# Softmax sums in a fused attention and convolution kernel: accumulated by DMA from GpSimd's queue in place of VectorE

## The chip, the cores and the metric

The kernel runs on one core of a Trainium2 chip. The metric is device time in microseconds (us) of one execution, taken as the median of several executions. The engines named below are TensorE (PE, with its weight loads as PEld), VectorE (DVE), ScalarE (ACT), GpSimd (POOL) and SyncE (SP, which here only issues DMAs). Each engine works through its own queue of instructions in order; an instruction that waits for a semaphore holds everything behind it on that engine.

## What is computed

Sixteen images of 128 channels and 32x32 positions (N = 1024) pass through two layers in float32.

```
qkv    = einsum('bchw,oc->bohw', x, w_qkv) + b_qkv          # 4 heads, 128 channels each
scores = einsum('bnc,bcm->bnm', q, k) * c ** (-0.5)
attn   = softmax(scores, axis=-1)
out    = einsum('bnm,bmc->bnc', attn, v)
x1     = einsum('bchw,oc->bohw', out, w_out) + b_out + x
# layer 1: two quantized 3x3 convolutions, each with batch norm over all images, and a residual
out    = batchnorm(conv3x3(act_quant(x1), weight_quant(w1)))
out    = batchnorm(conv3x3(act_quant(out), weight_quant(w2))) + x1
```

There are 64 heads (16 images by 4). The softmax divides by a sum over 1024 keys for every query; how these sums are formed is what the change is about.

## The kernel before, in words

**Attention (most of the time).** The weights are folded beforehand, so a head needs one projection `u` (L498) of the image, the scores `x^T u`, their exponentials, and a product with projected values `vo` (L520). For 63 of the 64 heads the loop at L902 runs four steps per head (`NK` = 4). A step takes two blocks of 128 keys: `scores` (L543) issues four score products of 512 queries on PE, and ACT writes their exponentials into one tile `e` of seven 128x512 slots (L551). The product with the values is done with seven half-size products instead of eight, so VectorE forms three combined operands from the four exponentials: T3 (L554), T1 and T2 in one instruction (L555), and T4 (L558). `attend` (L567) then issues the seven products into four PSUM banks. It does so one step late: in a step PE runs the scores of step s and then the products of step s-1.

**The sums.** T3 is B12+B22, the sum for the second half of the queries, and T4+T3 is B11+B21, the sum for the first half. So the sums over keys need only the slots T4 and T3, which are neighbours (`mine`, 128x1024). VectorE adds those of steps 0 and 1 into `sides[g]` (L562), and those of steps 2 and 3 on top (L564). At the end of the head `sum_up` (L634) reduces `sides[g]` over partitions in groups of 32 with one transposing reduce (L625). `inverse_sums` (L637) finishes the sum over the four partition groups with small copies (L652), a reduce (L654), an add (L657), a reciprocal (L658) and copies (L660), and spreads it over the partitions with a transpose (L664, tile `rb`).

**The rest of a head's end.** ACT copies the four PSUM banks out (`evacuate`, L595). `combine` (L601) alternates between ACT and VectorE: ACT copies L605 to L607, VectorE L608, ACT L612, VectorE L613, ACT L615, VectorE L617 and L618. `normalise` (L667) multiplies by `rb` and adds to the image's `acc` (L673 to L679). After an image's fourth head SP stores `acc` to DRAM (L681), and the image goes through quantization (L256, L257), row transforms (L782), the first convolution and its statistics between the steps of the next image's heads.

**What sets the order.** A dictionary `later` holds the work of head ends and other stages by step and half step (`at`, L846), and `run` calls it. That is the order in which the program is written; the framework that builds it may place an instruction earlier or later in its engine's queue, as long as the dependences hold. PE's products are chained in written order (`product`, L400).

**Buffers.** `e` has two buffers, so the first exponential of step s waits until every reader of step s-2's `e` is done. `es` (the accumulator `sides[g]`) has one, `u` two, the score PSUM tiles three. Since a step has four score products, the fourth product of a step needs the PSUM tile of the first, and so waits for the first exponential of that step.

**After attention.** Convolution outputs `ys` of the first layer stay in SBUF, except those of the images in `AWAY` (9 to 14, L240), which are stored to the DRAM tensor `y1d` (L813) and loaded back in one transfer, `back` (L987), before the second convolution.

Of the kernel before, what the change touches and what calls it, by code (L numbers as in the profile page):

```python
# [9 lines left out]
F32 = mybir.dt.float32  # L10
BF16 = mybir.dt.bfloat16
AF = mybir.ActivationFunctionType
ALU = mybir.AluOpType
# [178 lines left out]
def fast_path(  # L192
# [18 lines left out]
    B, C, N = x.shape  # L211
# [25 lines left out]
    for n in range(2):  # L237
        nc.gpsimd.memset(late[n][:, 0:1], float((B - 1) * N))

    AWAY = range(9, B - 1)  # L240
    ys = [None if b in AWAY else keep.tile([P, N], F32, name=f"y{b}") for b in range(B)]
    pads = []
    for i in range(NPAD):
# [4 lines left out]
    def quantize(b, src, scale, bias, r0=0, r1=H):  # L248

        cut = slice(r0 * W, r1 * W)  # L250
        t = qtp.tile([P, (r1 - r0) * W], F32, tag="qt", name="qt")
        if b == B - 1 and scale == A_LEVELS and r1 == H:
            nc.vector.tensor_scalar(t, src[:, cut], scale, 0.0, ALU.mult, ALU.max)
        else:
            nc.scalar.activation(t, src[:, cut], AF.Relu, bias=bias, scale=scale)
        nc.vector.tensor_scalar(t, t, A_LEVELS, MAGIC, ALU.min, ALU.add)  # L256
        return nc.vector.tensor_scalar(  # L257
            pads[b % NPAD][:, r0 + 1 : r1 + 1, 1 : W + 1],
            t.rearrange("p (h w) -> p h w", w=W),
            MAGIC,  # L260
            None,
            ALU.subtract,
        )
# [32 lines left out]
    def statistics(b, n):  # L296
        for hf in range(NHF):
            last = nc.vector.bn_stats(place(n, b, hf), ys[b][:, ts(hf, HALF)])  # L298
        return last
# [20 lines left out]
    def bn_params(n):  # L320

        new = lambda what: keep.tile([P, 1], F32, name=f"{what}{n}")
        mv = keep.tile([P, 2], F32, name=f"mv{n}")
        nc.vector.bn_aggr(mv, late[n])
        mean, var = mv[:, 0:1], mv[:, 1:2]
        rt = new("rt")
        nc.scalar.activation(rt, var, AF.Sqrt, bias=eps, scale=ss[:, n : n + 1])  # L327
        v = new("v")
        nc.vector.tensor_scalar(v, var, ss[:, n : n + 1], BN_EPS, ALU.mult, ALU.add)
        r = new("r")  # L330
        nc.vector.reciprocal(r, rt)

        t = new("t")
        nc.vector.tensor_scalar(t, r, r, v, ALU.mult, ALU.mult)
        nc.vector.tensor_scalar(t, t, -0.5, 1.5, ALU.mult, ALU.add)
        scale, bias = new("scale"), new("bias")
        nc.vector.tensor_scalar(scale, r, t, gs[:, n : n + 1], ALU.mult, ALU.mult)
        nc.vector.scalar_tensor_tensor(
            bias, mean, scale, be[:, n : n + 1], ALU.mult, ALU.subtract, reverse1=True
        )  # L340
        return scale, bias
# [31 lines left out]
    with ExitStack() as ph:  # L373
        pool = lambda name, bufs, **kw: ph.enter_context(tc.tile_pool(name=name, bufs=bufs, **kw))
# [2 lines left out]
        up = pool("u", 2)  # L377
        vp = pool("vo", 5)
        ep = pool("e", 2)
        esp = pool("es", 1)  # L380
        avp = pool("av", 1)
        evp = pool("ev", 1)
        smp = pool("small", 4)
# [11 lines left out]
        xt, us, vos, es, sides, avs, psa, accs, evs = {}, {}, {}, {}, {}, {}, {}, {}, {}  # L395
        exps, sums_added, attended, quantized, pe = [], [], [], [], []
# [120 lines left out]
        B12, B11, B22, B21, T4, T3, T2 = range(7)  # L517
# [22 lines left out]
        def score(ps, b, g, j, queries, cut=slice(0, HALF)):  # L540
            halves(ps[:, cut], lambda t: xt[b][:, ts(2 * j + t, PH)], us[g][:, queries])

        def scores(g, k, between=None):  # L543


            b, h = heads[g]
            e = es[g, k] = ep.tile([P, 7, HALF], F32, tag="e", name=f"e_{g}_{k}")
            for i, (c, m) in enumerate(((0, 1), (1, 1), (0, 0), (1, 0))):
                ps = ps_s.tile([P, HALF], F32, tag="s", name=f"pss_{g}_{k}_{i}")
                score(ps, b, g, k + NK * c, ts(m, HALF))  # L550
                exps[:] = [nc.scalar.activation(e[:, 2 * c + 1 - m], ps, AF.Exp).ins]  # L551
                if between and i in between:
                    between[i]()
            nc.vector.tensor_tensor(e[:, T3], e[:, B12], e[:, B22], ALU.add)  # L554
            nc.vector.tensor_tensor(  # L555
                e[:, T1 : T2 + 1 : T2 - T1], e[:, B12 : B11 + 1], e[:, B11 : T3 + 1 : T3 - B11], ALU.subtract
            )
            nc.vector.tensor_tensor(e[:, T4], e[:, T2], e[:, B21], ALU.add)  # L558
            mine = e[:, T4 : T3 + 1]
            if k == 1:  # L560
                sides[g] = esp.tile([P, NHF, HALF], F32, tag="es", name=f"es_{g}")
                nc.vector.tensor_tensor(sides[g], es[g, 0][:, T4 : T3 + 1], mine, ALU.add)  # L562
            elif k > 1:
                added = nc.vector.tensor_tensor(sides[g], sides[g], mine, ALU.add)  # L564
                sums_added[:] = [added.ins]

        def attend(g, k):  # L567
            b, h = heads[g]
# [231 lines left out]
        def rows_output(b):  # L800
            inner, others = ms.pop((b, True)), ms.pop((b, False))
            if b in AWAY:
                ys[b] = stp.tile([P, N], F32, tag="y", name=f"y_{b}")
# [6 lines left out]
        def first_statistics(b):  # L810
            statistics(b, 0)
            if b in AWAY:
                nc.sync.dma_start(out=y1d[b - AWAY.start], in_=ys[b])  # L813

# [31 lines left out]
        def at(step, half, fn, *args):  # L846

            later.setdefault(2 * step + half, []).append((fn, args))
# [21 lines left out]
        for g in range(LAST):  # L870
            b, h = heads[g]

            end = (g + 1) * NK
            at(end, 0, sum_up, g)
            at(end, 1, evacuate, g)
            at(end + 1, 0, combine, g, 0)
            at(end + 1, 1, combine, g, 1)
            at(end + 2, 0, combine, g, 2)
            at(end + 2, 1, normalise, g)
            if g > 0:  # L880
                at(g * NK + 1, 0, project_u, g + 1, 0)
                at(g * NK + 2, 0, project_u, g + 1, 1)
            if h == NH - 1:
                at(end + 3, 0, lambda b: quantize(b, accs[b], A_LEVELS, 0.0), b)
                at(end + 3, 1, sums_range, b)
                at(end + 4, 0, transform_rows, b)
                for i, k in enumerate((1, 2, 0, 3)):
                    at(end + 6 + (i + 1) // 2, (i + 1) % 2, rows_product, b, k)
                at(end + 8, 1, rows_output, b)
                at(end + 9, 0, first_statistics, b)  # L890
                if b + 2 < B:
                    at(end + 5, 0, load, b + 2, nc.scalar)
            elif h == NH - 2 and b + 1 < B:

                when = ((4, 0), (4, 1), (6, 1), (7, 0), (7, 1), (8, 0), (8, 1), (9, 1))
                for i, (step, half) in enumerate(when):
                    at(g * NK + step, half, project_v, b + 1, *divmod(i, 2))
# [4 lines left out]
        for step in range(n_steps):  # L902
            g, k = divmod(step, NK)
            between = {}
            if step == 1:
                banks = [ps_a.tile([P, HALF], F32, tag=f"a{2 + c}", name=f"psv_0_{c}") for c in range(2)]
                between = {0: lambda: project_v(0, 0, 0, banks[0]), 1: lambda: project_v(0, 0, 1, banks[1])}
            scores(g, k, between)
            if step == 0:
                fold_b()  # L910
            elif step < NK:
                project_v(0, step, 0)
            run(step, 0)
            if step > 0:
                attend(*divmod(step - 1, NK))
            if 0 < step < NK:
                ps = ps_s.tile([P, HALF], F32, tag="s", name=f"psv_0_{step}_1")
                project_v(0, step, 1, ps)
            run(step, 1)
# [31 lines left out]
    with ExitStack() as ph:  # L951
        pool = lambda name, bufs, **kw: ph.enter_context(tc.tile_pool(name=name, bufs=bufs, **kw))
# [32 lines left out]
        scale1, bias1 = bn_params(0)  # L985
        back = resp.tile([P, len(AWAY), N], F32, name="back")
        nc.sync.dma_start(out=back, in_=y1d.rearrange("b c n -> c b n"))  # L987
        for i, b in enumerate(AWAY):
            ys[b] = back[:, i]
# [203 lines left out]
def attention_then_quantized_convs(  # L1193
# [49 lines left out]
    def conv_weights(n, wp, behind):  # L1243
# [19 lines left out]

    flag = const.tile([1, 1], mybir.dt.int32, name="flag")
    fast_path(
        nc, tc, x, wqk, wvo, bo, bnp, x1d, y1d, out, bo_sb, bnp_sb, quad, wq, sc, flag, conv_weights,
        constants,
# [82 lines left out]
```

## Time and profile before

| what | value |
|---|---|
| three executions | 2024.09, 2026.29 and 2023.94 us; median 2024.09 us |
| span of the profiled execution (first to last instruction) | 2022.7 us |
| mean granted TensorE clock | 0.993 |
| PE busy | 1987.6 us (98%) |
| DVE busy | 1722.2 us (85%) |
| ACT busy | 1198.5 us (59%) |
| POOL busy | 19.7 us (1%) |
| DMA | 43.74 MB, mean 22 GB/s |

The profiled execution is one execution with its span; its own total time is not listed apart from the three runs, which lie 1.2 to 3.6 us above the span. A line of the page's table of groups names source line, engine, operation, output and inputs, count, busy time in us, mean ns of one instruction, and the idle time of the engine ahead of it. A line of the timeline gives start in us, length in us, engine, source line, operation and count, and in brackets how long the engine had been idle and who released it. A line of the waits gives who waited for whom, the total in us, the number of times and sometimes the longest.

### The profile page before, as it was taken

To read this page: it belongs to the slowest core of one execution; us is meant where nothing else is said; L and a number is where in the kernel's file an instruction comes from. 1 tells how busy PE (TensorE), PEld (TensorE's weight loads), DVE (VectorE), ACT (ScalarE), POOL (GpSimd) and SP (SyncE) were. 2 spreads that over 40 slices of the span, in tenths; PEclk is the share of its full clock that TensorE was granted. 3 is DMA by queue.
4 is the path that set the end of the run, shared out by engine and by line. 5 is a ranking of instruction groups with operands and counts; after the bars stand their busy time and mean duration, and the time that the engine had idled before them with its cause. 6 is when DMAs were issued, how large, how long until landed. Compare 5 with 4: busy or idle time off the path is not lost. (4 is left out here: it accounts for less than half of the span.)

```text
span 2022.7 us, 24701 instructions
## 1 busy us (share of the span) xinstructions
PE 1987.6 (98%) x9497; PEld 730.3 (36%) x9497; DVE 1722.2 (85%) x2642; ACT 1198.5 (59%) x2007; POOL 19.7 (1%) x29
## 2 busy tenths in 40 slices
PE   9999999999999999999999999999999999999994
PEld 3543333333333333333333333433333333333441
DVE  5889888888888888888888888888888888878888
ACT  4565665665566566566556556656656655655575
POOL 0000000000000000000000000000000000000020
PEclk9999999999999999999999999999999999999997
DMA  1000000000000000000000000000000000000064
GB/s 42 24 1 22 1 22 1 22 0 1 22 1 22 1 9 14 0 22 1 21 1 1 22 1 21 11 22 11 1 22 11 22 11 21 11 1 11 11 239 168
DMA packets 12846, 43.74 MB, mean 22 GB/s; under 512 B 1456, under 2 KB 1840, under 8 KB 12720
## 3 DMA queue, kind: packets, MB, share of 16 engines
q1 hardware_dynamic: 9520, 32.05, 4.2%
q10 hardware_dynamic: 3200, 10.03, 1.5%
q8 instruction: 76, 1.25, 0.3%
q14 instruction: 50, 0.41, 0.1%
HBM read 22.16 MB, written 19.92 MB: 21 GB/s over the span
## 5 line engine op out<-in xcount | busy, mean ns | idle before, releaser
L403 PE MATMUL pss<-u,x 128*64 128x512 f32 (+1 forms) x4128 | 1031.9, 589 | 1.6 <-ACT u L509 1.6
L403 PE MATMUL psa<-e,vo 128*64 128x512 f32 (+1 forms) x3624 | 922.4, 588 | 0.0
L551 ACT ACTIVATE e<-pss 128x512 f32<-128x512 f32 x1008 | 595.4, 596 | 380.7 <-PE pss L403 331.9
L403 PEld LDWEIGHTS pss<-u,x 128*64 128x64 f32 x4128 | 351.6, 137 | 549.3 <-issue 493.4
L403 PEld LDWEIGHTS psa<-e,vo 128*64 128x64 f32 x3624 | 304.8, 137 | 483.5 <-issue 449.6
L555 DVE TENSOR_TENSOR e<-e 128x1024 f32<-128x1024 f32 x252 | 307.7, 1221 | 29.8 <-ACT e L551 21.6
L554 DVE TENSOR_TENSOR e<-e 128x512 f32<-128x512 f32 x252 | 172.2, 683 | 105.5 <-ACT e L551 101.7
L558 DVE TENSOR_TENSOR e<-e 128x512 f32<-128x512 f32 x252 | 174.0, 690 | 21.5 <-DVE e L555 0.5
L595 ACT COPY ev<-psa 128x512 f32<-128x512 f32 x252 | 135.5, 589 | 87.2 <-PE psa L403 87.0
L403 PE MATMUL psu<-x,at_sb 128*64 128x512 f32 x512 | 184.9, 599 | 1.0 <-DMA x<-in_x_dram 1.0
L403 PE MATMUL psv<-bt_sb,x 128*64 128x512 f32 x512 | 184.9, 592 | 1.0 <-ACT bt_sb L480 1.0
L530 ACT COPY vo<-psv 128x512 f32<-128x512 f32 x128 | 75.5, 590 | 142.3 <-PE psv L403 142.3
L564 DVE TENSOR_TENSOR es<-es,e 128x1024 f32<-128x1024 f32 x126 | 154.0, 1222 | 2.7
L509 ACT ACTIVATE u<-psu,au_sb 128x512 f32<-128x512 f32 x127 | 87.4, 688 | 21.7 <-PE psu L403 20.1
L798 ACT ACTIVATE m<-psw 128x512 f32<-128x512 f32 x60 | 35.9, 598 | 92.6 <-PE psw L403 90.7
L608 DVE TENSOR_TENSOR y<-ev,y 128x512 f32<-128x512 f32 x63 | 43.6, 692 | 52.4 <-ACT y L606 52.4
L664 DVE STREAM_TRANSPOSE rb<-sums 128x1024 f32<-128x1024 f32 (+1 forms) x66 | 79.8, 1210 | 1.6
L625 DVE TRANSPOSE_TENSOR_REDUCE part<-es 128x32 f32<-128x1024 f32 (+1 forms) x65 | 79.6, 1224 | 1.1
L403 PEld LDWEIGHTS psv<-bt_sb,x 128*64 128x64 f32 x512 | 53.6, 137 | 73.5 <-issue 66.7
L403 PEld LDWEIGHTS psu<-x,at_sb 128*64 128x64 f32 x512 | 53.5, 138 | 73.1 <-issue 69.1
L562 DVE TENSOR_TENSOR es<-e,e 128x1024 f32<-128x1024 f32 x63 | 76.8, 1219 | 0.0
L675 DVE TENSOR_TENSOR av<-av,rb 128x1024 f32<-128x1024 f32 x47 | 57.6, 1225 | 1.6
(159 smaller groups left out, 1193.6 us busy)
## 6 DMA issues: line engine op xcount, KB each, us to landing
x_dram<-acc SPq DMA_DIRECT2D x16, 512.0 KB, 4.3
x<-in_x_dram ACTq DMA_DIRECT2D x15, 512.0 KB, 4.6
res<-x_dram SPq DMA_DIRECT2D x1, 7680.0 KB, 30.0
y_dram<-y SPq DMA_DIRECT2D x6, 512.0 KB, 2.6
back<-y_dram SPq DMA_DIRECT2D x1, 3072.0 KB, 11.4
out_dram<-back SPq DMA_DIRECT2D x6, 512.0 KB, 4.5
out_dram<-y SPq DMA_DIRECT2D x5, 512.0 KB, 4.1
out_dram<-y SPq DMA_DIRECT2D x9, 256.0 KB, 2.5
```

What stands on the lines that cost most here:

```text
L403: done = nc.tensor.matmul(out_, lhsT=lhsT, rhs=rhs, start=start, stop=stop)
L509: copied = nc.scalar.activation(dst, ps, AF.Identity, bias=au_sb[:, h : h + 1])
L530: nc.scalar.copy(v[:, c : c + 3 : 2], ps.rearrange("p (h a o) -> p a h o", a=2, o=PH))
L551: exps[:] = [nc.scalar.activation(e[:, 2 * c + 1 - m], ps, AF.Exp).ins]
L554: nc.vector.tensor_tensor(e[:, T3], e[:, B12], e[:, B22], ALU.add)
L555: nc.vector.tensor_tensor(e[:, T1 : T2 + 1 : T2 - T1], e[:, B12 : B11 + 1], e[:, B11 : T3 + 1 : T3 - B11], ALU.subtract)
L558: nc.vector.tensor_tensor(e[:, T4], e[:, T2], e[:, B21], ALU.add)
L562: nc.vector.tensor_tensor(sides[g], es[g, 0][:, T4 : T3 + 1], mine, ALU.add)
L564: added = nc.vector.tensor_tensor(sides[g], sides[g], mine, ALU.add)
L595: nc.scalar.copy(to, ps)
L625: nc.vector.tensor_reduce(part, total.rearrange("p (k c) -> p k c", c=Q), AX.X, ALU.add, apply_transpose=True,)
L664: nc.vector.transpose(rb, rinv.unsqueeze(2).to_broadcast([P, n, Q]))
```

## The change

The adds into the accumulator leave VectorE. Step 0's slots are copied into `sides[g]` by a DMA that SP issues. The slots of steps 1, 2 and 3 are added to it by DMAs that GpSimd issues with an accumulate operation; each moves 128x1024 floats, 512 KB, from SBUF to SBUF. Since they all write the same accumulator, each has to wait until the one before has landed. The accumulator gets a second buffer (4 KB of each partition), and the reduce over it, `sum_up`, is written one step later. The space comes from image 8, whose first convolution output now goes to DRAM as well (seven images in place of six).

```diff
-    AWAY = range(9, B - 1)
+    AWAY = range(8, B - 1)
...
-        esp = pool("es", 1)
+        esp = pool("es", 2)
...
-            nc.vector.tensor_tensor(e[:, T4], e[:, T2], e[:, B21], ALU.add)
+            last = nc.vector.tensor_tensor(e[:, T4], e[:, T2], e[:, B21], ALU.add)
             mine = e[:, T4 : T3 + 1]
-            if k == 1:
+            sums_added[:] = [last.ins]
+            if k == 0:
                 sides[g] = esp.tile([P, NHF, HALF], F32, tag="es", name=f"es_{g}")
-                nc.vector.tensor_tensor(sides[g], es[g, 0][:, T4 : T3 + 1], mine, ALU.add)
-            elif k > 1:
-                added = nc.vector.tensor_tensor(sides[g], sides[g], mine, ALU.add)
-                sums_added[:] = [added.ins]
+                nc.sync.dma_start(out=sides[g], in_=mine)
+            else:
+                nc.gpsimd.dma_start(out=sides[g], in_=mine, accum_op=ALU.add)
...
-            at(end, 0, sum_up, g)
+            at(end + 1, 0, sum_up, g)
...
-    args.append(nc.dram_tensor("y1_dram", (6, c, h * w), F32, kind="Internal").ap())
+    args.append(nc.dram_tensor("y1_dram", (7, c, h * w), F32, kind="Internal").ap())
```

In the changed kernel as it is built, the reduce L625 of a head stands in VectorE's queue directly after T4 of the head's last step (32 of 63 heads), or with two or three other instructions between (31 heads), and always ahead of T3 of the next head's first step.

## The prediction

> **What bounds the kernel now.** I read the page first: busy times, the slices, the costliest groups, the DMA issues.
>
> ```profile
> PE 1987.6 (98%) x9497; PEld 730.3 (36%) x9497; DVE 1722.2 (85%) x2642; ACT 1198.5 (59%) x2007; POOL 19.7 (1%) x29
> ...
> PE   9999999999999999999999999999999999999994
> ...
> DVE  5889888888888888888888888888888888878888
> ...
> L564 DVE TENSOR_TENSOR es<-es,e 128x1024 f32<-128x1024 f32 x126 | 154.0, 1222 | 2.7
> ...
> L562 DVE TENSOR_TENSOR es<-e,e 128x1024 f32<-128x1024 f32 x63 | 76.8, 1219 | 0.0
> ...
> y_dram<-y SPq DMA_DIRECT2D x6, 512.0 KB, 2.6
> ```
>
> PE is busy in every slice but the last. Its busy time is modelled, so I checked the pace of its weight loads in the timeline: from 113 us to the end of attention pairs follow each other every 0.43 us without a gap. VectorE has 15% idle, so attention is bound by PE, and VectorE matters only where something waits for it. Next the waits:
>
> ```profile
> ACT e L551 <- DVE es L562: 46.9, 46, 2.7
> ...
> PEld pss L403 <- ACT e L551: 17.8, 67, 0.7
> ```
>
> ACT waits for the first add of the sums 46 times, 1 us each, because L562 still reads step 0's `e` when step 2 needs that buffer. PE's loads behind ACT show 0.27 us a time, their ordinary gap. So that wait costs nothing: the score products run ahead by three PSUM tiles. Last, the timeline where head 17 ends and head 18 begins, a head of the second kind in an image:
>
> ```profile
> 551.61 0.69 DVE L558 TENSOR_TENSOR e<-e 128x512 f32<-128x512 f32 x1
> ...
> 554.56 1.24 DVE L625 TRANSPOSE_TENSOR_REDUCE part<-es 128x32 f32<-128x1024 f32 x1
> ...
> 565.60 3.17 PE L403 MATMUL psa<-e,vo 128*64 128x512 f32 x13
> ...
> 568.43 0.69 DVE L613 TENSOR_TENSOR y<-y,ev 128x512 f32<-128x512 f32 x1 [0.47 <-ACT ev L612]
> ...
> 569.16 0.61 ACT L615 COPY ev<-y 64x512 f32<-64x512 f32 x1 [0.76 <-DVE y L613]
> ...
> 570.35 1.20 ACT L551 ACTIVATE e<-pss 128x512 f32<-128x512 f32 x2 [0.58 <-DVE es L562]
> ```
>
> The chain to see: T4 of step 3 ends at 552.30; the reduce follows at 554.56; after it come the sums' tail and the next head's operands, until L613 lets ACT do L615, behind which the exponentials of step 2 stand in ACT's queue. Step 2's scores start at 568.60, and its fourth score product, six products of 0.43 us later at 571.17, needs the first exponential done. That must start by 570.5 (0.6 long, 0.05 for the hand-over). It starts at 570.35: 0.15 us in hand.
>
> [...]
>
> **The change, part by part.**
>
> *Removed:* 63 x 1.219 + 126 x 1.222 = 230.8 us of VectorE, 3.66 us a head, and ACT's 46.9 us of waits for L562. Worth 0 on the path, as PE has no gap to close. (The first 113 us have gaps, but for loads, weights and PSUM, not for these adds.)
>
> *Added on SP:* 63 copies of 512 KB, behind T4 of step 0; none is awaited before the first exponential of step 2, which in the example starts 8.3 us after that T4 (562.09 to 570.35). At 2.6 to 4.3 us (SP's 512 KB stores) it is hidden. Behind it on SP stand only the stores of `acc` and `y`, without a near reader. *On POOL:* 189 accumulates. Its two other instructions (maxima of the convolution weights) run at 57 and 87 us, and no accumulate is due while they wait. ACT waits for the accumulates when it needs `e` again two steps on: 6.7 us after T4 at the least, in most steps 7 to 10. *Image 8 in DRAM:* a 2.6 us store, hidden; `back` lands 11.4 x 7/6 = 13.3 us after 1928.3, at 1941.6, and is first read at 1951.2: 0.
>
> *Added wait, the step that decides:* L625 needs the last accumulate landed, and stands right behind T4 of step 3 in VectorE's queue. VectorE thus stands still for the whole latency A of that transfer, and behind it wait T3, T1/T2 and T4 of the next head, the tail of the sums and L608, L613. PE, ACT and the next accumulates wait for these. Writing `sum_up` one step later has not moved it behind them.
>
> A, from T4's end to L625's start: a store of the same size issued by SP takes 2.6. [...]queue q1 moved 32.05 MB in 4.2% of 16 engines' 2022.7 us, 23.6 GB/s per engine, so 512 KB take 1.4 us, and 1.4 more. [...]5.2, an estimate. Lower end 2.8 (SP's store plus hand-overs), upper 8 (the loaded store's 4.3 plus another 1.4[...]).
>
> Example, in the changed order: 552.30 + A; L625 1.27, four L652 0.76, L654 0.40, L657 0.20, L658 0.37, T3 0.67, L660 0.57, T1/T2 1.2, L664 1.17, T4 0.65, L808 1.25, L298 1.42, T3 0.64, L608 0.62, T1/T2 1.33, T4 0.65, L613 0.69: 13.9. L615 and hand-over 0.66. The first exponential of step 2 starts at 566.8 + A, limit 570.5: free up to A = 3.7.
>
> The other three kinds, in the same way:
> - First head of an image (16 to 17): T4 of step 3 ended at 525.82 behind a backlog; without two adds, but with L255 behind L679, I get 525.2. Chain 11.8, limit 540.4 (scores from 538.49): A = 3.4.
> - Third (14 to 15): 462.38, chain 12.1, limit 480.3: A = 5.8.
> - Fourth (15 to 16): 492.42, chain 13.4 with an L530, limit 512.9: A = 7.1.
>
> The next head's own products come later than this limit: T4 of step 0 would end at 559.6 + A, and is needed at 565.9.
>
> At A = 5.2 the first two kinds lose 1.8 + 1.5 = 3.3 us an image, in 15 whole images 49.5. A stall shifts PE, ACT and the exponentials together, so the next head begins from the same margin; nothing is paid back. Against the profiled execution: 2022.7 + 49.5 = 2072.2, and 1.4 outside the span (the median lies so far above it): 2073.6.
>
> **The rivals.** *Hidden after all (not slower):* the place is VectorE's idle time between T4 and the next T3, plus the 3.66 us freed per head. If A is at most 3.6, the worst kind loses 0.2 us, 15 x 0.2 = 3 us in all: 2024 to 2028. For it: SP's store of the same size lands in 2.6[...]. Against: both are plain copies. *Slow accumulates:* if A is 8, it exceeds a step (119.24 us for an image's 16 steps: 7.45). Each waits for its predecessor, so the third lags by 2 x 0.55 more, 9.1 in effect; losses 5.7 + 5.4 + 3.3 + 2.0 = 16.4 an image, 246 us: 2270. For it: an adding unit's rate in float32 is nowhere shown. *A gain:* VectorE's freed 231 us would have to reach PE; no gap speaks for it, and the tail (from 1950 us) keeps its VectorE work.
>
> **How the numbers follow.** Forecast, A between 3.6 and 7: 0.70. Hidden: 0.16, of which 0.03 for a gain over 0.2% (4 us, about what a measurement of this kernel can tell from no change). Slow accumulates, A over 7: 0.14. At A = 7: 3.6 + 3.3 + 1.2 = 8.1 an image, 122 us: 2146, the upper end. The lower end, 2022, takes in the hidden case; left out are 0.14 and 0.03. Slower 0.84, same 0.13, faster 0.03.
>
> **What would show it.** L625 idle before each time by about A less the instructions between, waiting for DMA, 63 times; A as time to landing of the POOL-issued transfers plus about 0.3. PE gaps of 1 to 2 us at the fourth score product of step 2 in first and second heads, none in the fourth; ACT waiting for L613 ahead of them. VectorE busy 231 us less. I would be wrong if PE shows no gaps though L625 waits (margins miscounted), if ACT's exponentials wait for DMA on `e` (buffers decide), or if L625 barely waits.

## The result, and the profile after

The changed kernel takes 2060.86 us (median of 4 runs, 2059.87 to 2062.36) against 2024.01 us for the kernel before (4 runs, 2022.53 to 2026.29). The ratio is 1.0182, with a 95% interval from 1.0169 to 1.0194. It is slower by 36.9 us; the forecast was slower by 49.5 us. The profiled execution took 2060.91 us with a span of 2059.0 us, so spans differ by 36.3 us.

The page of the changed kernel, its busy times, the slices of PE and VectorE, three groups, and the DMA issues:

```profile
PE 2007.1 (97%) x9496; PEld 819.9 (40%) x9497; DVE 1491.4 (72%) x2453; ACT 1191.1 (58%) x2007; POOL 182.8 (9%) x218
...
PE   9999999999999999999999999999999999999994
...
DVE  3867776876777677677777677677667767767888
...
L403 PE MATMUL pss<-u,x 128*64 128x512 f32 (+1 forms) x4128 | 1050.3, 592 | 18.6 <-ACT e L551 16.0
...
L565 POOL DMA_DIRECT2D es<-e x189 | 163.0, 863 | 1737.3 <-DVE e L558 1623.2
...
L625 DVE TRANSPOSE_TENSOR_REDUCE part<-es 128x32 f32<-128x1024 f32 (+1 forms) x65 | 79.8, 1228 | 287.4 <-DMA es<-e 287.4
...
es<-e POOLq DMA_DIRECT2D x189, 512.0 KB, 4.5
es<-e SPq DMA_DIRECT2D x63, 512.0 KB, 2.9
...
y_dram<-y SPq DMA_DIRECT2D x7, 512.0 KB, 3.1
back<-y_dram SPq DMA_DIRECT2D x1, 3584.0 KB, 12.8
```

VectorE has lost 230.8 us of work (1722.2 to 1491.4) and stands still for 287.4 us in front of one line, L625. PE's slices look as before: a loss of 2% in an engine that is 97% busy doesn't show in tenths. It shows in the waits (engine, what it waited for: us in all, times, longest). The first four lines are those of the changed kernel, the last is that of the kernel before:

```profile
DVE part L625 <- DMA es<-e: 287.4, 63, 6.6
...
ACT ev L615 <- DVE y L613: 71.1, 46, 1.9
...
PEld pss L403 <- ACT e L551: 52.7, 65, 4.1
...
PE pss L403 <- ACT e L551: 16.0, 22, 3.2
...
ACT ev L615 <- DVE y L613: 23.1, 30, 1.1
```

Read it as a chain from the top: VectorE waits for the last accumulate 63 times; ACT waits for L613 48 us more than before (71.1, before 23.1); PE's weight loads for scores wait for exponentials 35 us more (52.7, before 17.8), and no longer at their ordinary 0.27 us a time. ACT's 46.9 us of waits for L562 are gone. No line has the exponentials waiting for a transfer that still reads `e`, so the buffers do not decide.

The timeline shows one case from end to end, heads 9 and 10, a second head of an image as in the prediction's example:

```profile
323.78 0.69 DVE L558 TENSOR_TENSOR e<-e 128x512 f32<-128x512 f32 x1
...
324.76 0.86 POOL L565 DMA_DIRECT2D es<-e  x1 [6.39 <-DVE e L558]
...
329.30 1.25 DVE L625 TRANSPOSE_TENSOR_REDUCE part<-es 128x32 f32<-128x1024 f32 x1 [3.63 <-DMA es<-e]
...
341.88 0.68 DVE L613 TENSOR_TENSOR y<-y,ev 128x512 f32<-128x512 f32 x1
...
342.60 0.61 ACT L615 COPY ev<-y 64x512 f32<-64x512 f32 x1 [1.92 <-DVE y L613]
...
343.24 1.58 ACT L551 ACTIVATE e<-pss 128x512 f32<-128x512 f32 x3
...
343.89 1.08 PE L403 MATMUL pss<-u,x 128*64 128x512 f32 x4 [0.22 <-ACT e L551]
```

T4 ends at 324.47; GpSimd issues the transfer 0.3 us later; the reduce starts at 329.30. So A, the time from T4's end to L625, is 4.83 us here. L613 comes 12.58 us after L625, then ACT's copy and the exponential, then PE. The weight loads say what PE lost: ordinarily a pair follows the one before after 0.29 us, and here the gap is 0.80 us longer. I call this the excess gap, and added up all of them. Between 115 and 1950 us they are 31.9 us in the changed kernel and 0.6 before: 14.0 in first heads of an image, 17.5 in second heads, and none in third and fourth heads but one of 0.4 that the kernel before has too.

A second count closes the sum. The weight loads come in the same order in both kernels, so I compared when the load of the same number starts. By 115 us (on the clock of the kernel before) the changed kernel is 7.6 us late, and by 1902 us, near the end of attention, 36.0 us; the spans differ by 36.3. Between the two points it is 28.4 us, somewhat less than the gaps: a gap is 0.1 us (first heads) to 0.2 us (second heads) longer than the delay that it leaves.

### The profile page after: what moved, and what is told of

Read it like the earlier page. It is cut to its first block, busy times and chain, and to the rows that moved or that the text cites. A ratio compares the mean times of both kernels' runs of the same rounds, so it can differ in the third digit from the quotient of the medians.

```text
span 2059.0 us, 25183 instructions
## 1 busy us (share of the span) xinstructions
PE 2007.1 (97%) x9496; PEld 819.9 (40%) x9497; DVE 1491.4 (72%) x2453; ACT 1191.1 (58%) x2007; POOL 182.8 (9%) x218
## 3 DMA queue, kind: packets, MB, share of 16 engines
q0 software_dynamic: 27216, 99.10, 25.4%
## 4 chain that ended last, share of the span: by engine, by line
PE 67%; DVE 16%; ACT 6%; DMA 5%; issue 5%; POOL 0%; DVEq 0%; SPq 0%; POOLq 0%; ACTq 0%
PE pss L403 29%; PE psa L403 27%; DMA es<-e 5%; PE psv L403 5%; DVE e L555 4%; PE psu L403 4%; ACT e L551 3%; DVE e L558 2%; PE psc L282 1%; PE psw L403 1%; DVE e L554 1%; DVE y L613 1%; DVE rb L664 1%; DVE early L298 1%; ACT ev L595 1%
## 5 line engine op out<-in xcount | busy, mean ns | idle before, releaser
L403 PE MATMUL pss<-u,x 128*64 128x512 f32 (+1 forms) x4128 | 1050.3, 592 | 18.6 <-ACT e L551 16.0
L551 ACT ACTIVATE e<-pss 128x512 f32<-128x512 f32 x1008 | 588.6, 595 | 344.5 <-PE pss L403 313.7
L403 PEld LDWEIGHTS pss<-u,x 128*64 128x64 f32 x4128 | 379.6, 137 | 543.1 <-issue 459.9
L403 PEld LDWEIGHTS psa<-e,vo 128*64 128x64 f32 x3624 | 335.7, 137 | 463.6 <-issue 430.8
L565 POOL DMA_DIRECT2D es<-e x189 | 163.0, 863 | 1737.3 <-DVE e L558 1623.2
L625 DVE TRANSPOSE_TENSOR_REDUCE part<-es 128x32 f32<-128x1024 f32 (+1 forms) x65 | 79.8, 1228 | 287.4 <-DMA es<-e 287.4
L403 PE MATMUL psu<-x,at_sb 128*64 128x512 f32 x512 | 177.4, 603 | 0.4 <-DMA x<-in_x_dram 0.4
L615 ACT COPY ev<-y 64x512 f32<-64x512 f32 x63 | 38.8, 616 | 72.2 <-DVE y L613 71.1
L676 DVE TENSOR_TENSOR acc<-acc,av 128x1024 f32<-128x1024 f32 x47 | 57.5, 1224 | 1.5
## 6 DMA issues: line engine op xcount, KB each, us to landing
back<-y_dram SPq DMA_DIRECT2D x1, 3584.0 KB, 12.8
```

What stands on the lines that cost most here:

```text
L403: done = nc.tensor.matmul(out_, lhsT=lhsT, rhs=rhs, start=start, stop=stop)
L565: nc.gpsimd.dma_start(out=sides[g], in_=mine, accum_op=ALU.add)
L625: nc.vector.tensor_reduce(part, total.rearrange("p (k c) -> p k c", c=Q), AX.X, ALU.add, apply_transpose=True,)
```

## The experiments

The theory to be tested: the loss is VectorE's standstill in front of L625, A less what a head has free. The rivals: the transfers' traffic slows PE or ACT; the transfers hold `e`; image 8 in DRAM or SP's longer queue cost something. Each ratio below is to 32 or 39 runs of the kernel before, taken beside the experiment (medians 2024.5 and 2024.4 us).

**The reduce put behind the next head's T4.** The transfers stay, the wait goes.

```diff
-            sides[g] = quadrant_sums(sides[g].rearrange("p a n -> p (a n)"))
+            with tc.issue_after(sums_added[0]):
+                sides[g] = quadrant_sums(sides[g].rearrange("p a n -> p (a n)"))
...
-            at(end + 1, 0, sum_up, g)
+            at(end, 0, sum_up, g)
```

> The changed kernel with one thing more: the reduce L625 is bound to stand behind T4 of the next head's step 0 in VectorE's queue (47 of 63 heads right behind it, 15 with one instruction between). Transfers, buffers and sums stay as they are. My theory (VectorE's standstill at L625 costs the time): a step lasts 7.45 us and the last accumulate takes 4.85 from T4 to the reduce, so L625 no longer waits for DMA, the stalls of PE at the fourth score product of step 2 go, and so does most of the 36.9 us: 2024 to 2032 us, the upper part if the 5.1 us lost in head 2 come from something else. Rival (the accumulates' traffic in SBUF slows PE or ACT): no change, 2058 to 2062. Rival (e buffers are held by transfers): no change, 2058 to 2062.

Measured: 2025.18 us, ratio to the kernel before 1.0005 (0.9996 to 1.0014). The excess gaps after 115 us are 0.6 us, as before the change. Its waits:

```profile
ACT ev L615 <- DVE y L613: 29.4, 36, 1.7
...
DVE part L625 <- DMA es<-e: 7.4, 5, 5.9
```

The reduce waits 7.4 us in all where it waited 287.4, with the same 189 transfers landing in the same 4.5 us. One instruction's place in VectorE's queue holds the loss; what the transfers do to others does not. Even the 5.1 us that the changed kernel lost in head 2 (below) went down to 0.9.

**The accumulates as plain copies.** This parts what the addition costs from what GpSimd's issue costs.

```diff
-                nc.gpsimd.dma_start(out=sides[g], in_=mine, accum_op=ALU.add)
+                nc.gpsimd.dma_start(out=sides[g], in_=mine)
```

> The changed kernel with GpSimd's 189 transfers as plain copies, without the addition (the sums then hold only the last step's part; the rest of the computation is the same). Same queue, same order on VectorE, same writes[...]. [...] My theory: only the time from T4 to L625 counts. Estimate from SP's copies of the same size in the changed kernel (2.9 us from issue to landing) and the 0.3 us from T4 to GpSimd's issue: 3.2 to 3.9, below the 4.05 us free in second heads and the 4.7 in first heads, so 2024 to 2032. If instead the path through GpSimd makes most of the 4.5 us, the transfers still land in 4 us or more, and a part of the loss stays: 2035 to 2060. Rival (traffic): a third less of it, so two thirds of the loss stay, about 2049.

Measured: 2029.32 us, ratio 1.0023 (1.0014 to 1.0031). Its groups and DMA issues:

```profile
L625 DVE TRANSPOSE_TENSOR_REDUCE part<-es 128x32 f32<-128x1024 f32 (+1 forms) x65 | 79.8, 1228 | 173.9 <-DMA es<-e 173.9
L565 POOL DMA_DIRECT2D es<-e x189 | 100.8, 533 | 1768.8 <-DVE e L558 1745.7
...
es<-e POOLq DMA_DIRECT2D x189, 512.0 KB, 2.9
es<-e SPq DMA_DIRECT2D x63, 512.0 KB, 2.9
```

GpSimd's plain copy lands in 2.9 us, exactly as SP's. So GpSimd's issue adds nothing that can be seen, and the addition makes the whole difference in landing, 1.7 us (4.54 against 2.86 before rounding). The trace's DMA packets split it. The first packet starts 1.10 us after GpSimd's issue here (SP's: 1.12) and 1.43 us after it with the addition; these 0.33 us are what GpSimd's instruction is longer. From the first packet to the last it is 1.43 us here and 2.78 us with the addition, 1.35 us more. A falls to 3.15 to 3.22 us in most heads and nearly all gaps go: VectorE still waits 173.9 us in front of L625, and this costs nothing. What is left are two late transfers (A of 5.4 and 5.8, gaps of 1.1 and 1.5 us, in second heads) and 2.1 us in head 2.

**The traffic alone.** VectorE adds as before the change; beside it all 252 transfers go into an accumulator that nobody reads, and image 8 goes to DRAM (its lines are not shown).

```diff
+            if k == 0:
+                unread[:] = [esp.tile([P, NHF, HALF], F32, tag="un", name=f"un_{g}")]
+                nc.sync.dma_start(out=unread[0], in_=mine)
+            else:
+                nc.gpsimd.dma_start(out=unread[0], in_=mine, accum_op=ALU.add)
```

> The kernel before, its sums added by VectorE as ever, and beside them all of the change's 252 transfers (63 SP copies, 189 GpSimd accumulates) into an accumulator that nobody reads; image 8 in DRAM as in the change. So the traffic, GpSimd's issuing and the hold on the e buffers are there, and VectorE waits for none of it. My theory: 2024 to 2028. Rivals (traffic in SBUF, e buffers held, image 8, SP's queue): all of their cost is here too, 2045 to 2062.

Measured: 2023.80 us, ratio 0.9995 (0.9987 to 1.0004). The transfers landed in 4.5 us as in the changed kernel, and the excess gaps after 115 us are 0.6 us. All the rivals' costs were in this run, and together they are nothing that can be measured.

**The wait doubled.** A second accumulate behind that of step 3; the lines that write the reduce earlier and bind T3 of the next head behind it are not shown.

```diff
+            if k == NK - 1:
+                nc.gpsimd.dma_start(out=sides[g].rearrange("p a n -> p (a n)"), in_=xt[b], accum_op=ALU.add)
```

> The changed kernel with a second accumulate behind that of step 3 in every head, reading the image's x (so the sums are wrong by x; the rest is the same), and the reduce bound ahead of the next head's T3 so that it keeps its place. The scheduler then puts part of the sums' tail behind L613, which I work out as 2.3 us less between L625 and L613 in first and second heads, 1.2 in third and 0.6 in fourth. My theory: the wait from T4 to L625 grows from 4.85 to about 9.35 us, free are 7.0, 6.35, 7.0 and 7.7 us in the four heads of an image, so they lose 2.9, 3.0, 2.4 and 1.7 us: 10 us an image, 150 in 15, with the start-up's 8 about 2180 us (2130 to 2240), and PE stalls in third and fourth heads too. Rival (traffic): a third more accumulates, a third more of the 37 us, about 2073.

Measured: 2308.08 us, ratio 1.1397 (1.1378 to 1.1416). The direction is the theory's and the traffic rival is out by more than 200 us, but the size is 128 us above my 2180. Its waits say why:

```profile
DVE part L629 <- DMA es<-x: 643.2, 63, 13.1
...
PEld psa L404 <- DVE e L560: 175.8, 57, 6.7
...
PE psa L404 <- DVE e L560: 128.9, 49, 5.9
```

Three things were missed. A is not 9.35 but 9.7 to 13 us, since T4 of steps 2 and 3 are 3.7 to 4.6 us apart in many heads and the accumulates of a head wait for one another. And another wait ends last: PE's own products of the next head (`psa`) wait for T4 of its step 0 (L560 here). That limit stands in the prediction (T4 would end at 559.6 + A, needed at 565.9, so 6.3 us are free), and I had left it out of this expectation. In the excess gaps of this run it is 154 us; the chain to the exponentials has 47, and 41 more stand where PE waits for ACT's `u` ahead of `psv`. Last, behind some stalls the pairs of loads come at half their pace for a time (see the last section): behind one of 5.65 us that ended at 96.55, every 0.85 us in place of 0.43 until 101.6. By the gaps this comes to 35 us.

**The last part by VectorE.** Steps 1 and 2 stay accumulates.

```diff
-            else:
+            elif k < NK - 1:
                 nc.gpsimd.dma_start(out=sides[g], in_=mine, accum_op=ALU.add)
+            else:
+                nc.vector.tensor_tensor(sides[g], sides[g], mine, ALU.add)
```

> The changed kernel with the part of step 3, the last of each head, added by VectorE again; steps 1 and 2 stay accumulates of GpSimd, step 0 SP's copy. The add waits for the accumulate of step 2, which was issued a step earlier (4.6 to 8 us before), so little of its 4.85 us is left. My theory: 2024 to 2029 us, L625 waiting for nothing, VectorE about 77 us busier than with the change. Rival (it is the number of transfers, or what they do to SBUF or to the e buffers): a third of them is gone, so two thirds of the 37 us stay, about 2049.

Measured: 2025.01 us, ratio 1.0002 (0.9995 to 1.0009). A third of the accumulates is gone, but all of the loss. The two groups of its page:

```profile
L567 DVE TENSOR_TENSOR es<-es,e 128x1024 f32<-128x1024 f32 x63 | 77.0, 1222 | 10.7 <-DMA es<-e 10.1
...
L627 DVE TRANSPOSE_TENSOR_REDUCE part<-es 128x32 f32<-128x1024 f32 (+1 forms) x65 | 79.6, 1225 | 1.1
```

The add waits 10.1 us in all for the accumulate of step 2, which has a step's time to land. These 77 us of VectorE's work cost nothing, where the wait in front of L625 cost 37 us.

**The last accumulate later by a small copy.** As in the run with the wait doubled, the lines that keep VectorE's order are not shown.

```diff
+                if k == NK - 1:
+                    nc.gpsimd.tensor_copy(smp.tile([P, 256], F32, tag="un", bufs=1, name=f"un_{g}"), e[:, T4, 0:256])
                 nc.gpsimd.dma_start(out=sides[g], in_=mine, accum_op=ALU.add)
```

> The changed kernel with a small GpSimd copy (128x256 float32 out of T4 into an unread tile) ahead of the last accumulate of each head, which so goes out later by the copy's time d; T3 of the next head is bound behind the reduce, so that VectorE's order stays nearly as it was. It gives the slope at the working point. My theory: first and second heads of an image are both past their margins, so the time grows by 2 d an image, 30 d in 15 images; third heads join in from a wait of 5.8 us on. The copy's time is nowhere in the traces; at 0.5 to 1.2 us it gives 2076 to 2097, or more if third heads join. Rival (traffic): 1 per cent more bytes, no change: 2061.

Measured: 2059.98 us, ratio 1.0174 (1.0157 to 1.0191), the same as the changed kernel. The expectation failed, because the copy (0.49 us on average) did not do to A what I took for granted. In second heads A rose from 4.87 to 5.35. In first heads it fell from 5.36 to about 5.14: there the transfer otherwise waits for the one before it, and the copy lay in that time. That A fell, and didn't only stay, shows in GpSimd's own waits: in the changed kernel a transfer that waits for its predecessor goes out 0.53 us after that one has landed (17 times), but with the copy in between GpSimd comes to it only after the landing, and it goes out as soon as the copy ends, some 0.3 us after the landing. Why the wait itself costs these 0.2 us is not shown. The losses followed A in both. Each pair below is A and the excess gap of one head, from the two kernels:

| | changed kernel | with the copy |
|---|---|---|
| first heads | 5.36: 0.67; 6.65: 1.94 | 5.14: 0.44; 5.37: 0.66; 6.60: 1.89 |
| second heads | 4.81: 0.79; 5.71: 1.67; 6.92: 2.67 | 5.33: 1.22; 7.49: 3.35 |

First heads lose A less 4.7 us, second heads A less 4.05 us, with 0.2 to either side. So the law of the prediction holds with a slope of one and different margins, and the sum over the image happened to stay: excess gaps are 33.5 us against 31.9.

**VectorE's backlog brought back.** The adds of steps 1 and 2 are done as well, into a tile that nobody reads (the lines that send image 7 to DRAM are not shown).

```diff
                 nc.gpsimd.dma_start(out=sides[g], in_=mine, accum_op=ALU.add)
+            if k == 1:
+                unread[:] = [esp.tile([P, NHF, HALF], F32, tag="un", bufs=1, name=f"un_{g}")]
+                nc.vector.tensor_tensor(unread[0], es[g, 0][:, T4 : T3 + 1], mine, ALU.add)
+            elif k == 2:
+                nc.vector.tensor_tensor(unread[0], unread[0], mine, ALU.add)
```

> The changed kernel with VectorE's adds of steps 1 and 2 done as well, into a tile that nobody reads (image 7 goes to DRAM too, for the room). The true sums still come by the transfers. In the changed kernel T4 of step 3 in first heads ended 1.19 us after the fourth exponential; in the kernel before it was 2.84, since VectorE was behind with its work. My theory: with the adds back the backlog returns, first heads lose up to 1.65 us more of their margin: 10 to 25 us in 15 images, 2070 to 2086. If first heads' margin doesn't hang on the freed work: 2061. Rival (transfers themselves cost the time): 2061.

Measured: 2123.52 us, ratio 1.0479 (1.0462 to 1.0497), well above my 2086. Here is a first head, 12, and the next one's steps:

```profile
425.06 0.68 DVE L559 TENSOR_TENSOR e<-e 128x512 f32<-128x512 f32 x1
...
430.61 1.25 DVE L631 TRANSPOSE_TENSOR_REDUCE part<-es 128x32 f32<-128x1024 f32 x1 [4.86 <-DMA es<-e]
...
440.78 0.68 DVE L619 TENSOR_TENSOR y<-y,ev 128x512 f32<-128x512 f32 x1
...
441.38 1.22 DVE L569 TENSOR_TENSOR un<-e,e 128x1024 f32<-128x1024 f32 x1
441.50 0.61 ACT L621 COPY ev<-y 64x512 f32<-64x512 f32 x1 [1.92 <-DVE y L619]
...
442.69 1.57 ACT L552 ACTIVATE e<-pss 128x512 f32<-128x512 f32 x3 [0.57 <-DVE un L569]
```

The backlog is back to the hundredth: T4 of step 3 ends 2.84 us after the fourth exponential, as before the change (2.83), and not 1.19 as in the changed kernel. That is 1.65 us of margin. The kernel before, at the end of head 16 (the exponential ends at 522.98, T4 at 525.81):

```profile
522.38 0.60 ACT L551 ACTIVATE e<-pss 128x512 f32<-128x512 f32 x1 [0.26 <-PE pss L403]
...
525.13 0.68 DVE L558 TENSOR_TENSOR e<-e 128x512 f32<-128x512 f32 x1
```

The last line of head 12's timeline shows a second price that I had not counted: the exponential waits 0.57 us more, for L569, which reads the `e` that it will write. Both together take a first head's margin from 4.7 to 2.5 us (gap 2.34 at A = 4.86) and a second head's from 4.05 to 3.5. Third heads, which lost nothing in the changed kernel, lose 0.8 each: there the exponential waits for L569 too (1.8 us in head 10). So the freed VectorE time did help the changed kernel, by the 63 us that this run loses against it, but only against the wait that the same change brought in.

**The accumulates in halves.** T3's half goes out when T3 is there.

```diff
             nc.vector.tensor_tensor(e[:, T3], e[:, B12], e[:, B22], ALU.add)
+            if k > 0:
+                nc.gpsimd.dma_start(out=sides[g][:, 1], in_=e[:, T3], accum_op=ALU.add)
...
-                nc.gpsimd.dma_start(out=sides[g], in_=mine, accum_op=ALU.add)
+                nc.gpsimd.dma_start(out=sides[g][:, 0], in_=mine[:, 0], accum_op=ALU.add)
```

> The changed kernel with each accumulate cut in two of 256 KB: T3's half goes out when T3 is there, ahead of T1, T2 and T4; only T4's half is left after T4. Twice as many GpSimd transfers, the same bytes. My theory: what counts is the time from T4 to L625. The accumulate of 512 KB lands 4.5 us after issue, GpSimd's plain copy of it 2.9; an accumulate of half the size should save about half of the 1.6 us that adding costs and of the bytes' own time, so 4.0 or less from T4 to L625, below the 4.05 us of second heads: 2024 to 2032. If T4's half has to wait for T3's half, which accumulates into the other half of the tile, A stays near 4.9 and the time near 2061. Rival (the number of transfers, or GpSimd's issuing): 2061 or more.

Measured: 2026.52 us, ratio 1.0010 (1.0003 to 1.0017). Its DMA issues and GpSimd's two lines:

```profile
L556 POOL DMA_DIRECT2D es<-e x189 | 164.2, 869 | 1275.3 <-DVE e L554 862.8
...
L567 POOL DMA_DIRECT2D es<-e x189 | 165.4, 875 | 267.7 <-DVE e L560 247.2
...
es<-e POOLq DMA_DIRECT2D x378, 256.0 KB, 3.3
```

The half lands in 3.3 us, A is 3.65 to 3.70 in most heads of all four kinds, below both margins, and nearly all gaps go. Twice as many transfers cost less than one that lands 1.2 us later. No kernel here beats the kernel before: PE had no gap to give.

## Why the prediction was right, and where its sizes were off

**PE is the bound, so 230.8 us of VectorE are worth nothing.** Right. With the waits taken out (the reduce moved, or the last part by VectorE) VectorE is 138 to 226 us less busy than before the change, and the time is that of before.

**The added wait decides.** Right, and shown from both sides: moving L625 alone gives 2025 us, the same transfers with nobody waiting for them 2024. L625 waits for DMA 63 times. The rival "hidden after all" needed A up to 3.6 and is what the plain copies and the halves show; at 4.85 it is out. Slow accumulates, A over 7, are out by the same figure; of the 8 us named for them, 2.3 were a guess of mine.

**A = 5.2 us.** Measured 4.8 to 4.9 in ordinary second, third and fourth heads and 5.3 to 5.5, mostly 5.36, in first heads. The parts were off in ways that nearly cancelled, which was luck. Beside the 2.6 of SP's store and the 1.4 more for the addition, A held 1.2 us for GpSimd's path and the hand-overs, a guess of mine that no trace of before supports. GpSimd's path adds nothing in the plain copies: the first packet starts 1.10 us after GpSimd's issue and 1.12 after SP's. The base was 2.9 where I had taken 2.6. The 1.4 more, which assumed that adding doubles the time of the bytes, is 1.35 by the packets. Of the 1.2, 0.33 went into GpSimd's longer issue and 0.3 into the hand-over from T4. The profile's shares of queue q0 agree with the doubling: for the same 27216 packets and 99.10 MB the DMA engines were busy about twice as long, first the changed kernel, then the plain copies:

```profile
q0 software_dynamic: 27216, 99.10, 25.4%
...
q0 software_dynamic: 27216, 99.10, 12.1%
```

What in the adding takes the time, no run separates. In first heads T4 of steps 2 and 3 are only 4.57 us apart, less than A, so the last transfer waits 0.5 us for its predecessor. Head 16 of the changed kernel shows it (T4 ends at 537.17):

```profile
536.48 0.69 DVE L558 TENSOR_TENSOR e<-e 128x512 f32<-128x512 f32 x1
...
537.99 0.86 POOL L565 DMA_DIRECT2D es<-e  x1 [4.23 <-DMA es<-e]
```

The prediction has this lag, but only under the rival of slow accumulates: the spacing of T4s in each head, not a step's mean of 7.45, had to be compared with A.

**Margins of 3.4, 3.7, 5.8 and 7.1 us.** Measured 4.7 and 4.05 for first and second heads; third and fourth lost nothing at an A of up to 5.2. This is the step that was mis-sized, above all in first heads. I had let the freed work bring T4 forward by 0.6 us (525.82 to 525.2); it came 1.65 us sooner, as the backlog vanished altogether. That is 1.05 of the 1.3 us by which the margin of first heads was short. The rest is the chain from L625 to L613, where I had added single durations: instructions on VectorE overlap by some 0.06 us each (above, L619 starts at 440.78, takes 0.68 us, and L569 starts at 441.38), and the chain is 12.58 us in second heads where I had 13.2. There 0.3 of these 0.6 us are missing again in the measured margin, in part because it is worked out from gaps, which overstate the delay by 0.2. So first heads lose 0.67 us, not 1.8, and second heads 0.80, not 1.5: 1.5 us of gaps an image, 22 us in 15, where the forecast had 49.5.

**What the sum had missed.** Some 9 us of gaps: in seven heads the last transfer is late (A from 5.3 to 6.9, gaps up to 2.67 us), which comes to 7.8 us over the ordinary gaps, and head 61 has a longer chain to L613 (1.2 us). In six of the seven the last transfer or the one before it took 5.0 to 5.8 us to land; why stays open. In the seventh, head 37, GpSimd's 114th transfer goes out 2.3 us after T4 where 0.3 is usual. In all nine kernels with such transfers it is the 114th that goes out late, 2.3 to 2.9 us after T4, wherever it stands: in head 37 with three transfers in a head, 28 with four, 56 with two, 18 with six halves. So it goes by the count, not by the place or the bytes: queue q0 has 144 packets a transfer, of 512 KB (27216 in 189) and of 256 KB (54432 in 378) alike. Why it is the 114th, no run shows.

And the first 115 us lose 7.6 us, which I had put at nothing. 5.1 of them fall in head 2. There VectorE does the convolution weights in the chain to L613, so its margin is smaller (the timeline of the changed kernel):

```profile
95.57 0.75 DVE L1256 TENSOR_SCALAR raw<-raw 128x1152 f32<-128x1152 f32 x1
...
97.61 0.69 DVE L613 TENSOR_TENSOR y<-y,ev 128x512 f32<-128x512 f32 x1
...
99.62 1.98 PE L403 MATMUL pss<-u,x 128*64 128x512 f32 x4 [3.24 <-ACT e L551]
```

The wait there is of the same kind: 3.8 us of excess gap here, 0.9 with the reduce moved, none with the last part by VectorE; a slower pace follows it (last section). Another 0.7 us come at 51 us, where PE waits for weights that VectorE forms behind the first L625. The other 1.8 us, at 10 us into the kernel, are not the change's: the traced executions of four experiments have them, the unread transfers among them, and those of the other four have not.

**Nothing for SP's copies, `e`, image 8 and POOL's maxima.** Right, as the unread transfers show: 0.9995. `back` landed in 12.8 us, 13.3 were forecast.

**Which heads stall.** Right: first and second, not the third and fourth; at the fourth score product of step 2, ahead of which ACT waits for L613. The gaps are 0.6 to 1 us in most, below the 1 to 2 that I named.

## What to carry to other kernels

Where an engine hands work to a DMA and reads the result itself, ask what stands behind the reader in its queue. Here the 231 us of freed time were worth nothing, since VectorE was not the limit, and the reader's wait, 287.4 us in all, was paid by all that stood behind it, less the margin of each place. Put the reader behind work that doesn't need it, or hand over only parts that have a step's time to land. When you work out a margin, take the order of work after the change: work that is removed also removes backlog ahead of the place, and the spacing of the transfers in that place decides whether they queue.

## What the runs showed of the hardware

- An accumulate in float32 from SBUF to SBUF, 512 KB, issued by GpSimd, lands 4.5 us after issue; 256 KB 3.3 us; a plain copy of 512 KB 2.9 us from GpSimd and from SP alike. From the first packet to the last it is 2.78 us for the accumulate of 512 KB and 1.43 us for GpSimd's copy.
- GpSimd is busy 0.86 us per accumulate of 512 KB and 0.87 us at 256 KB, 0.53 us per plain copy: half the bytes in as many rows (128) cost it as much.
- 252 such transfers, 132 MB in all, beside 2024 us of matmuls, adds and exponentials cost nothing that can be measured (ratio 0.9987 to 1.0004).
- GpSimd's 114th transfer goes out about 2 us late in every one of nine kernels.
- The stall in head 2 cost more than itself. After it PE's pairs of weight loads came every 0.85 us for 3 us and then every 0.43 again (the timeline of the changed kernel):

```profile
99.62 0.30 PEld L403 LDWEIGHTS pss<-u,x 128*64 128x64 f32 x4 [4.12 <-ACT e L551]
100.53 0.24 PEld L403 LDWEIGHTS psu<-x,at_sb 128*64 128x64 f32 x2 [0.61 <-issue]
101.39 0.24 PEld L403 LDWEIGHTS psu<-x,at_sb 128*64 128x64 f32 x2 [0.61 <-issue]
102.24 0.24 PEld L403 LDWEIGHTS psa<-e,vo 128*64 128x64 f32 x2 [0.61 <-DVE av L675]
102.94 0.14 PEld L403 LDWEIGHTS psa<-e,vo 128*64 128x64 f32 x2 [0.47 <-issue]
103.38 0.14 PEld L403 LDWEIGHTS psa<-e,vo 128*64 128x64 f32 x2 [0.29 <-issue]
```

That is half the pace, and the trace's granted clock is 0.50 from 99.6 to 102.3 us. In the same kernel it is 1.00 from 115 to 1950 us, with excess gaps of up to 2.67 us. In two other runs the slower pace followed a wait of the loads of 4.12 us (with the copy, for 3 us) and one of 5.65 us (with the wait doubled, for 5 us); waits of 2.63 and 2.85 us, with the backlog brought back, were followed by a pair every 0.43 us. How long a stall has to be does not follow from these runs. With the wait doubled, where the loads waited for L560 57 times and up to 6.7 us, the mean granted clock was 0.967, in the changed kernel 0.992.
